# The last 64 tokens of layer 1's attention: from a padded tile of their own rows and columns to units of two halves

## The chip, the core and the metric

The kernel runs on one core of a Trainium2 chip. The metric is the device time of one execution in microseconds (us). The engines that matter are TensorE (PE in the profile, with its weight loads as PEld), VectorE (DVE), ScalarE (ACT), GpSimd (POOL), and SyncE (SP), on whose queue the large transfers are issued. [...]

## The reference

Four layers work on an image batch of 4 x 56 x 56 tokens with 256 channels. Each adds to x what a group-normalised x yields. The change concerns layer 1, whose attention is over all T = 3136 tokens of an image:

```python
xn = x / jnp.maximum(jnp.linalg.norm(x, axis=-1, keepdims=True), EPS)
A = jnp.einsum('bnc,cc,bmc->bnm', xn, W_adj, xn)
A = jnp.exp(5.0 * (A - jnp.max(A, axis=-1, keepdims=True)))
A = A * (1.0 - jnp.eye(n, dtype=A.dtype))
A = A / jnp.maximum(jnp.sum(jnp.abs(A), axis=-1, keepdims=True), EPS)
rowsum = jnp.sum(A, axis=-1, keepdims=True)
xW = jnp.einsum('bnc,dc->bnd', x, W_aff)
Ax = jnp.einsum('bnm,bmc->bnc', A, x)
AxW = jnp.einsum('bnc,dc->bnd', Ax, W_aff)
diff = rowsum * (xW + b_aff) - AxW
...
y = (diff - mu) * jax.lax.rsqrt(var + LN_EPS) * ln_gamma + ln_beta
y = jnp.where(y > 0, y, LEAK * y)
```

W_adj enters by its diagonal alone, so A before its division is symmetric.

## The kernel before

**Tiles.** Tokens are cut into tiles of P = 128. T is 24 whole tiles and 64 tokens more, so NB is 25, and tile 24 is filled up with zeros. Per image the kernel holds `xnT`, the tokens of unit length with channels on partitions (two halves of 128 channels), and `xw`, x times W_aff with tokens on partitions and a 257th column of -1, which yields the row sums.

**Units.** As A is symmetric, only its upper triangle is computed. Row j of tiles runs from tile j to tile 24 in units of up to four tiles (`units`): 25 rows, 91 units and 325 pairs of tiles per image, 300 of them of different tiles. A unit has these steps:

- `logits`: two matmuls (one per channel half, L1377) of up to 512 columns into the PSUM buffer `s`, the exponential on ACT (L1380) into `e`; in a diagonal tile the own token is taken out on POOL (L1382). The stationary side, `xd`, is xnT times the diagonal of W_adj, made on POOL (`scaled`, L1370).
- `transposed`: PE transposes the tiles that are not on the diagonal into `ps_t` (L1391), ACT copies them to `at` (L1394).
- `products`: for each tile two matmuls of 257 columns. `by_row` (L1405) adds to row j's sum in the PSUM buffer `o`. `by_column` (L1410) makes row i's share in the PSUM buffer `v`, which DVE adds to `acc` in SBUF (L1414; in row 0 a copy, L1412). `o`, `s` and `v` have two buffers each.

After a row's last unit `finish` closes the row: DVE adds `o` and `acc` (L1441), divides (L1444, L1446), makes statistics (L1449 to L1451), waits for POOL's power (L1453), scales (L1454), waits for POOL's gamma and beta (L1455, L1456) and applies the leak (L1457). Its second half, `add`, transposes y on PE (L1462) and adds it to the residual (L1470), which is stored when a seventh of the image is complete (L1473).

**Tokens.** `tokens(b, c)` brings in a chunk c of four tiles of image b: load (L1323), normalise (L940), square, `lengths` (L1336, with POOL's power L1339 and the diagonal matrix `dg` L1340), `values` (L1349, evacuated by L953 and L955) and `unit_length` (L1357, then DVE's write of xnT, L1359). Chunk 6 is the 64 tokens alone. Image 0's chunks come first. A later image's chunks are written over those that the rows before have used up: `replace` loads chunk c and puts its steps into the list `small`, from which `small_step` takes one step twice in each unit when it is due; `there` forces the steps of a chunk that the next unit needs. Chunk 6 of an image is replaced in row 0 of that image itself.

**Order.** In layer 1 PE's order is the order of the source. The other engines' orders come from a planner. The main loop works one unit ahead: transposes of unit k, logits of unit k + 1, products of unit k.

```python
            small_step()
            at = transposed(*w, e)
            ...
            if k + 1 < len(units):
                there(units[k + 1][0], units[k + 1][3] - 1)
                ahead = logits(*units[k + 1])
            small_step()
            products(*w, e, at)
            done += last - first
            if last == NB:
                small.append((done + 6, finish(b, j), None))
```

Of the kernel before, what the change touches and what calls it, by code (L numbers as in the profile page):

```python
# [24 lines left out]
FP = mybir.dt.float32  # L25
# [806 lines left out]
def direct_blocks(ctx: ExitStack, tc: tile.TileContext, d: dict, watch):  # L832
# [463 lines left out]

    def layer1(early, big, pool, brief):
        NB = -(-T // P)  # L1300
        real = lambda i: min(P, T - i * P)
        nonlocal m_bufs
        m_bufs, ps_a = 1, ps_m
        w_aff = weight(early, "waff", C)
        acc = big.tile([P, NB, C + 1], FP, name="acc")
        xnT = big.tile([P, CC, NB * P], FP, name="xnT")
        xw = big.tile([P, NB, C + 1], FP, name="xw")
        offd = big.tile([P, P], FP, name="offd")
        nc.vector.tensor_scalar(offd, ident, -1.0, 1.0, ALU.mult, ALU.add)
        nc.vector.memset(xw[:, :, C:], -1.0)  # L1310
        nc.vector.memset(xw[T % P:, NB - 1, :], 0.0)
        nc.vector.memset(xnT[:, :, T:], 0.0)

        def tokens(b, c, ps_a=ps_m):

            tiles = range(4 * c, min(4 * c + 4, NB))
            n = sum(real(t) for t in tiles)
            k, m = real(tiles[0]), len(tiles)
            box = {}

            def load():
                x = early.tile([P, CC, 512], FP, tag="x", name="x1")
                nc.sync.dma_start(out=x[:, :, :n], in_=tokens_of(1, b, 4 * c * P, n))  # L1323
                x1 = box["x"] = early.tile([P, CC, 512], FP, tag="xn", name="xn1")
                sq = box["sq"] = early.tile([P, CC, 512], FP, tag="sq", name="sq", bufs=1)
                for h in range(CC):
                    normalise(x1[:, h, :n], x[:, h, :n], known(1, b), h)
                nc.scalar.activation(sq[:, :, :n], x1[:, :, :n], AF.Square)

            def lengths():  # L1330
                pm, sq = ps_a(), box["sq"]
                rn = early.tile([P, 4, 1], FP, tag="rn", name="rn")
                dg = box["dg"] = early.tile([P, 4, P], FP, tag="dg", name="dg", bufs=1)
                for i, t in enumerate(tiles):
                    for h in range(CC):
                        nc.tensor.matmul(pm[:k, i:i + 1], lhsT=sq[:, h, i * P:i * P + k], rhs=ones[:, 0:1],  # L1336
                                         start=(h == 0), stop=(h == CC - 1))
                nc.vector.tensor_scalar_max(rn[:k, :m, 0], pm[:k, :m], TINY * TINY)
                nc.gpsimd.tensor_tensor(rn[:k, :m, 0], rn[:k, :m, 0], mhalf[:k, 0:1].to_broadcast([k, m]), ALU.pow)  # L1339
                nc.gpsimd.tensor_tensor(  # L1340
                    dg[:k, :m, :k], ident[:k, :k].rearrange("p (o q) -> p o q", o=1).to_broadcast([k, m, k]),
                    rn[:k, :m, :].to_broadcast([k, m, k]), ALU.mult)

            def values(i0):
                pm = ps_a()
                mm = min(2, m - i0)
                for i in range(i0, i0 + mm):
                    for h in range(CC):
                        nc.tensor.matmul(pm[:k, (i - i0) * C:(i - i0 + 1) * C], lhsT=box["x"][:, h, i * P:i * P + k],  # L1349
                                         rhs=w_aff[:, h, :], start=(h == 0), stop=(h == CC - 1))  # L1350
                evac(i0 // 2, xw[:k, 4 * c + i0:4 * c + i0 + mm, :C],
                     pm[:k, :mm * C].rearrange("p (a b) -> p a b", b=C))

            def unit_length():

                pm = ps_a()
                nc.tensor.matmul(pm[:, :n].rearrange("p (m k) -> p m k", k=k), lhsT=ones[:k, :], rhs=box["dg"][:k, :m, :k],  # L1357
                                 start=True, stop=True)
                nc.vector.tensor_tensor(xnT[:, :, 4 * c * P:4 * c * P + n], box["x"][:, :, :n],  # L1359
                                        pm[:, :n].rearrange("p (o k) -> p o k", o=1).to_broadcast([P, CC, n]), ALU.mult)  # L1360

            return [load, lengths] + [lambda i=i: values(i) for i in range(0, m, 2)] + [unit_length]

        xd, out, xr = {}, {}, {}

        def scaled(j):

# [4 lines left out]
        def logits(b, j, first, last):  # L1372

            n = (last - first) * P
            s = psum_tile("s", 2)
            for h in range(CC):
                nc.tensor.matmul(s[:, :n], lhsT=xd[j][:, h, :], rhs=xnT[:, h, first * P:last * P],  # L1377
                                 start=(h == 0), stop=(h == CC - 1))
            e = pool.tile([P, 512], FP, tag="e", name="e1", bufs=3)
            nc.scalar.activation(e[:, :n], s[:, :n], AF.Exp, scale=5.0)  # L1380
            if first == j:
                nc.gpsimd.tensor_tensor(e[:, :P], e[:, :P], offd, ALU.mult)  # L1382
            return e

        def transposed(b, j, first, last, e):
            at = pool.tile([P, 512], FP, tag="at", name="at1")
# [10 lines left out]
        def products(b, j, first, last, e, at):  # L1397
# [10 lines left out]
            def by_column(i):  # L1408
                pv = psum_tile("v", 2)
                nc.tensor.matmul(pv[:, :C + 1], lhsT=e[:, col(i)], rhs=xw[:, j, :], start=True, stop=True)  # L1410
                if j == 0:
                    nc.vector.tensor_copy(acc[:, i, :], pv[:, :C + 1])  # L1412
                else:
                    nc.vector.tensor_tensor(acc[:, i, :], acc[:, i, :], pv[:, :C + 1], ALU.add)  # L1414

            rows = list(range(first, last))
            if first == j:
# [5 lines left out]
            for i in rows:  # L1423
                by_row(i)

        def residual(b, c):

            if (b, c) not in xr and c < NCH:
# [3 lines left out]

        def finish(b, j):

            n = real(j)
            y = pool.tile([P, C + 1], FP, tag="y", name="y", bufs=5)
            u = pool.tile([P, C], FP, tag="u", name="u")
            rd = pool.tile([P, 1], FP, tag="rd", name="rd")
            nc.gpsimd.tensor_tensor(u[:n], xw[:n, j, :C], baff[:n], ALU.add)
            if j:  # L1440
                nc.vector.tensor_tensor(y[:n], out[j][:n, :C + 1], acc[:n, j, :], ALU.add)  # L1441
            else:
                nc.vector.tensor_copy(y[:n], out[j][:n, :C + 1])
            nc.vector.reciprocal(rd[:n], y[:n, C:])  # L1444
            y = y[:n, :C]
            nc.vector.scalar_tensor_tensor(y, y, rd[:n], u[:n], ALU.mult, ALU.add)  # L1446
# [12 lines left out]
            def add():  # L1459
# [5 lines left out]
                while t0 < j * P + n:  # L1465
# [2 lines left out]
                    x = residual(b, c)  # L1468
                    xv = x[:, :, t0 - c * CH:t1 - c * CH]
                    nc.vector.tensor_tensor(xv, xv, pt[:, :, t0 - j * P:t1 - j * P], ALU.add)  # L1470
                    if t1 == (c + 1) * CH:
                        add_stats(2, b, c, x)
                        nc.sync.dma_start(out=tokens_of(2, b, c * CH, CH), in_=x)  # L1473
                    t0 = t1
# [1 line left out]

        NC4 = -(-NB // 4)
        units = [(b, j, i, min(i + 4, NB)) for b in range(NIMG) for j in range(NB) for i in range(j, NB, 4)]  # L1480
        turn = iter(range(4 * NC4))
        fresh = [tokens(0, c, lambda: psum_tile(*(("v", 2), ("o", 2), ("t", 1), ("s", 2))[next(turn) % 4])) for c in range(NC4)]
        for c in range(2):
            fresh[c].pop(0)()
        for c in range(NC4):
            for step in fresh[c]:
                step()
            if c + 2 < NC4:
                fresh[c + 2].pop(0)()
        scaled(0)  # L1490
        e = logits(*units[0])
        small, done = [], 0

        def small_step():
# [3 lines left out]
                    return step()  # L1498
            step_stats()

        def there(b, tile):

            for item in [a for a in small if a[2] == (b, tile // 4)]:
                small.remove(item)
                item[1]()

        def replace(b, c):
            load, *steps = tokens(b, c)
            load()
            at = sum(a[2] is not None for a in small)  # L1510
            small[at:at] = [(done + 8, step, (b, c)) for step in steps]

        for k, w in enumerate(units):
            b, j, first, last = w
            if first == j:
                residual(b, j * P // CH)
                residual(b, j * P // CH + 1)
                if b + 1 < NIMG and j % 4 == 2 and j >= 6:
                    replace(b + 1, j // 4 - 1)
                if b + 1 < NIMG and j == NB - 1:  # L1520
                    replace(b + 1, NC4 - 2)
                if b and j == 0:
                    replace(b, NC4 - 1)
            small_step()
            at = transposed(*w, e)
            if k + 2 < len(units) and units[k + 2][1] == units[k + 2][2]:
                scaled(units[k + 2][1])
            if k + 1 < len(units):
                there(units[k + 1][0], units[k + 1][3] - 1)
                ahead = logits(*units[k + 1])  # L1530
            small_step()
            products(*w, e, at)
            done += last - first
            if last == NB:
                small.append((done + 6, finish(b, j), None))
            e = ahead
        for _, step, _ in small:
            step()
# [491 lines left out]
```

## Time and profile before

| | |
|---|---|
| median of 3 runs | 4114.57 us (4113.07 to 4121.27) |
| profiled execution | 4111.69 us, its span 4109.9 us |
| busy share of the span | PE 95%, PEld 68%, DVE 58%, ACT 33%, POOL 42% |
| mean granted TensorE clock | 0.981 |
| DVE additions to acc (L1414) | 1104, 457.2 us |
| ACT copies of transposes (L1394) | 360, 184.8 us |
| ACT exponentials (L1380) | 364, 200.8 us |

A busy time of PE is the union of its matmuls, whose ends are modelled and overlap. In a group the columns are: line, engine, operation, output and inputs, shape, count, busy time, mean time of one in ns, and the idle time of the engine before them with what ended most of it. In PE's shapes 128*128 stands for rows and columns of the array that an instruction uses. Layer 1 lies between about 825 and 2850 us from the start of the span.

### The profile page before, as it was taken

How to read it: one execution, taken by the hardware profiler on the slowest of the kernel's cores; microseconds unless marked ns; L12 is line 12 of the kernel's file. 1: busy time of each engine (PE TensorE's matmuls, PEld its weight loads, DVE VectorE, ACT ScalarE, POOL GpSimd, SP SyncE). 2: the span in 40 equal slices, each digit the busy share in tenths (PEclk: the TensorE clock that was granted, in tenths of full speed). 3: DMA queues.
4: the chain of work that ended last, by engine and by line, in shares of the span. 5: the costliest groups of instructions: out<-in, count | busy, mean ns of one | idle time of the engine just before them, and what ended most of it. 6: DMA issues, size and time to landing. Idle time of an engine off the chain costs nothing. (4 is left out here: it accounts for less than half of the span.)

```text
span 4109.9 us, 92570 instructions
## 1 busy us (share of the span) xinstructions
PE 3910.4 (95%) x39191; PEld 2788.9 (68%) x39191; DVE 2381.8 (58%) x4437; ACT 1373.1 (33%) x2850; POOL 1741.2 (42%) x1883
## 2 busy tenths in 40 slices
PE   6899999899999999999999999997999999899998
PEld 4566666577777677776777677775666666666665
DVE  6777777734345434454344533444688887666665
ACT  2444545422222122221222212222554555444443
POOL 2566667621123211242112411123676777554544
PEclk9999999999999999999999999998999999999999
DMA  7344333210000100000000000003344443322221
GB/s 261 101 133 122 113 112 101 89 41 10 15 15 24 34 9 15 15 29 29 10 15 15 28 17 10 10 19 117 109 127 121 123 122 112 104 76 73 72 76 61
DMA packets 239794, 275.89 MB, mean 67 GB/s; under 512 B 22150, under 2 KB 231720, under 8 KB 238888
## 3 DMA queue, kind: packets, MB, share of 16 engines
q1 hardware_dynamic: 239082, 269.80, 21.1%
q8 instruction: 310, 5.08, 0.5%
q14 instruction: 114, 0.93, 0.1%
q10 hardware_dynamic: 288, 0.08, 0.0%
HBM read 190.29 MB, written 79.53 MB: 66 GB/s over the span
## 5 line engine op out<-in xcount | busy, mean ns | idle before, releaser
L1414 DVE TENSOR_TENSOR acc<-acc,ps_v 128x257 f32<-128x257 f32 x1104 | 457.2, 421 | 679.5 <-PE ps_v L1410 676.6
L1410 PE MATMUL ps_v<-xw,e 128*128 128x257 f32 x2400 | 666.4, 382 | 27.4 <-DVE acc L1414 17.2
L1405 PE MATMUL ps_o<-xw,at 128*128 128x257 f32 x2400 | 662.5, 380 | 0.0
L1377 PE MATMUL ps_s<-xnT,xd 128*128 128x512 f32 (+3 forms) x1456 | 622.0, 550 | 5.1 <-DVE xnT L1359 5.1
L1410 PEld LDWEIGHTS ps_v<-xw,e 128*128 128x128 f32 x2400 | 445.1, 189 | 193.2 <-issue 91.8
L1394 ACT COPY at<-ps_t 128x512 f32<-128x512 f32 (+3 forms) x360 | 184.8, 513 | 1054.4 <-PE ps_t L1391 1054.4
L1064 POOL TENSOR_TENSOR b<-e 126x336 f32<-126x336 f32 (+5 forms) x512 | 499.7, 997 | 12.1 <-ACT e L1052 4.1
L1405 PEld LDWEIGHTS ps_o<-xw,at 128*128 128x128 f32 x2400 | 455.5, 190 | 65.3
L1370 POOL TENSOR_SCALAR xd<-xnT,vec 128x128 f32<-128x128 f32 x200 | 122.2, 622 | 707.4 <-PE ps_s L1377 705.6
L946 PE MATMUL ps_m<-xn,w_wqkv 128*128 128x392 f32 x1024 | 375.5, 500 | 3.3 <-DVE xr L1693 2.5
L1055 POOL TENSOR_TENSOR e<-e,m0t 126x672 f32<-126x672 f32 (+3 forms) x128 | 238.7, 1865 | 280.7 <-ACT e L1054 267.9
L1377 PEld LDWEIGHTS ps_s<-xnT,xd 128*128 128x128 f32 x1456 | 245.1, 191 | 155.6 <-issue 138.8
L1055 POOL TENSOR_TENSOR e<-e,bias 119x784 f32<-119x784 f32 (+5 forms) x128 | 244.5, 1911 | 215.7 <-ACT e L1054 214.8
L1380 ACT ACTIVATE e<-ps_s 128x512 f32<-128x512 f32 (+3 forms) x364 | 200.8, 552 | 375.2 <-PE ps_s L1377 373.3
L976 ACT ACTIVATE no<-rs 128x168 f32<-128x168 f32 (+2 forms) x256 | 93.8, 367 | 624.7 <-DVE rs L1658 283.1
L1073 PEld LDWEIGHTS ps_o<-e,vp 124*32 124x32 f32 (+3 forms) x8192 | 177.1, 111 | 142.9 <-issue 93.5
L946 PEld LDWEIGHTS ps_m<-xn,w_wqkv 128*128 128x128 f32 x1024 | 188.2, 190 | 124.8 <-ACT pr L1886 17.3
L963 PE MATMUL ps_m<-w_wqkv,xn 128*98 128x256 f32 x1024 | 250.0, 388 | 8.2 <-DMA w_wqkv<-in_wqkv 7.0
L1073 PE MATMUL ps_o<-e,vp 124*32 124x112 f32 (+3 forms) x8192 | 240.2, 254 | 6.2 <-POOL e L1055 4.7
L940 DVE TENSOR_SCALAR xn<-x,gst 128x28 f32<-128x28 f32 (+5 forms) x368 | 204.8, 611 | 50.7 <-PE ps_m L946 26.9
L1052 ACT ACTIVATE e<-e 126x672 f32<-126x672 f32 (+5 forms) x256 | 219.4, 857 | 24.0 <-DVE e L1051 10.7
L965 DVE TENSOR_TENSOR v<-ps_m,bc 98x512 f32<-98x512 f32 (+1 forms) x184 | 126.2, 686 | 174.3 <-PE ps_m L963 98.3
(164 smaller groups left out, 6136.4 us busy)
## 6 DMA issues: line engine op xcount, KB each, us to landing
x<-xr SPq DMA_DIRECT2D x64, 392.0 KB
x<-in_x SPq DMA_DIRECT2D x53, 448.0 KB
xr<-x SPq DMA_DIRECT2D x60, 392.0 KB
x<-x SPq DMA_DIRECT2D x60, 392.0 KB
vd<-v SPq DMA_DIRECT2D x28, 448.0 KB
xr<-in_x SPq DMA_DIRECT2D x32, 392.0 KB
xr<-x SPq DMA_DIRECT2D x28, 448.0 KB
x<-xr SPq DMA_DIRECT2D x28, 448.0 KB
```

What stands on the lines that cost most here:

```text
L940: nc.vector.tensor_scalar(dst, src, gst[:, h, 0:1], gst[:, h, 1:2], ALU.subtract, ALU.mult)
L946: nc.tensor.matmul(pm[:, :n], lhsT=w[:, h, col:col + P], rhs=rhs(h), start=(h == 0), stop=(h == CC - 1))
L963: nc.tensor.matmul(pm[:n, j * C:(j + 1) * C], lhsT=xn[:, h, k * n:(k + 1) * n], rhs=w[:, h, :], start=(h == 0), stop=(h == CC - 1))
L1052: nc.scalar.activation(ev, ev, AF.Exp)
L1055: nc.gpsimd.tensor_tensor(parts(ev), parts(ev), w["emask"], ALU.mult)
L1064: nc.gpsimd.tensor_tensor(w["b"][a][:nk, :, :2 * nq].rearrange("p h (i c) -> p h i c", i=2), ev[:, :, :, 0, :], ev[:, :, :, 1, :], ALU.add)
L1073: nc.tensor.matmul(w["o"](k, i)[j * HD:(j + 1) * HD], lhsT=ones[:nk, :HD] if k else v(j, u), rhs=w["b"][j // 2][:nk, j % 2, i * nq:(i + 1) ...
L1377: nc.tensor.matmul(s[:, :n], lhsT=xd[j][:, h, :], rhs=xnT[:, h, first * P:last * P], start=(h == 0), stop=(h == CC - 1))
L1380: nc.scalar.activation(e[:, :n], s[:, :n], AF.Exp, scale=5.0)
L1405: nc.tensor.matmul(out[j][:, :C + 1], lhsT=e[:, col(i)] if i == j else at[:, col(i)], rhs=xw[:, i, :], start=(i == j), stop=(i == NB - 1))
L1410: nc.tensor.matmul(pv[:, :C + 1], lhsT=e[:, col(i)], rhs=xw[:, j, :], start=True, stop=True)
L1414: nc.vector.tensor_tensor(acc[:, i, :], acc[:, i, :], pv[:, :C + 1], ALU.add)
```

## The change

Rows and units now cover the 24 whole tiles alone (84 units, 276 pairs of different tiles and 24 diagonal ones per image). The 64 tokens are handled *by row* in three units of their own per image, each of which takes eight whole tiles: two halves of four tiles side by side.

- The 64 tokens are loaded twice, so that chunk 6 is a whole tile with two equal halves; `xdr` is its scaled copy. Both halves of `xw` and `xnT` of tile 24 are real data.
- `rest_logits`: half a of the array's columns takes the 64 tokens against tiles 8q + 4a to 8q + 4a + 3. One PSUM buffer holds both, one exponential serves both.
- `rest_transposed`: four transposes, each of which turns two tiles.
- `rest_products`: in four steps, the shares of two tiles (`by_column`'s work, on the two row halves of the array) into both `v` buffers, and the rest's own sums (`by_row`'s work, on the two column halves) into one `o` buffer, whose halves are added later through `racc`.
- `add_up` copies to `acc` at an image's first touch of a tile and adds after that; of the copies of a rest unit the second goes to ACT.
- The last unit also has the 64 tokens among themselves (`own`), and after it `finish(b, NB)` closes their row. Its `add` comes with that of row 23.
- Order: image 0 starts with units 0 and 1 of the rest; those of a later image stand behind rows 20 and 21 of the image before; unit 2 stands behind row 0. `replace` takes chunk 6 at row 3, 0 to 3 at rows 6, 10, 14, 18, 4 at row 20 and 5 at row 22, puts new steps at the head of `small`, and first does what is left of earlier chunks.

```diff
+            if (b, i) in touched:
+                nc.vector.tensor_tensor(acc[:, i, :], acc[:, i, :], pv[:, :C + 1], ALU.add)
+            else:
+                touched.add((b, i))
+                copy(acc[:, i, :], pv[:, :C + 1])
+        def rest_logits(q):
+            s = psum_tile("s", 2)
+            for a in range(2):
+                for h in range(CC):
+                    nc.tensor.matmul(s[a * REST:(a + 1) * REST, :], lhsT=xdr[:, h, a * REST:(a + 1) * REST],
+                                     rhs=xnT[:, h, (2 * q + a) * 512:(2 * q + a + 1) * 512], start=(h == 0), stop=(h == CC - 1))
+            e = pool.tile([P, 512], FP, tag="e", name="e1", bufs=3)
+            nc.scalar.activation(e, s, AF.Exp, scale=5.0)
...
+        def rest_products(b, q, e, own, at):
+            po = psum_tile("o", 2)
+            for i in range(4):
+                pv = [psum_tile("v", 2) for a in range(2)]
+                for a in range(2):
+                    half = slice(a * REST, (a + 1) * REST)
+                    nc.tensor.matmul(pv[a][:, :C + 1], lhsT=e[half, i * P:(i + 1) * P], rhs=xw[half, NB, :], start=True, stop=True)
+                for a in range(2):
+                    add_up(b, 8 * q + 4 * a + i, pv[a], (nc.vector.tensor_copy, nc.scalar.copy)[a])
+                for a in range(2):
+                    nc.tensor.matmul(po[a * REST:(a + 1) * REST, :C + 1], lhsT=at[:, i * P + a * REST:i * P + (a + 1) * REST],
+                                     rhs=xw[:, 8 * q + 4 * a + i, :], start=(i == 0), stop=(i == 3 and (a == 1 or own is None)))
...
+            if q == 0:
+                nc.vector.tensor_copy(racc, po[:, :C + 1])
+            else:
+                nc.vector.tensor_tensor(racc, racc, po[:, :C + 1], ALU.add)
...
+        units = []
+        for b in range(NIMG):
+            if b == 0:
+                units += [(b, None, q) for q in range(2)]
+            for j in range(NB):
+                units += [(b, j, i, min(i + 4, NB)) for i in range(j, NB, 4)]
+                if j == 0:
+                    units.append((b, None, 2))
+                if b + 1 < NIMG and 0 <= j - 20 < 2:
+                    units.append((b + 1, None, j - 20))
...
-                if b + 1 < NIMG and j % 4 == 2 and j >= 6:
-                    replace(b + 1, j // 4 - 1)
-                if b + 1 < NIMG and j == NB - 1:
-                    replace(b + 1, NC4 - 2)
-                if b and j == 0:
-                    replace(b, NC4 - 1)
+                if j in (3, 6, 10, 14, 18, 20, 22):
+                    replace(b + 1, {3: NC4, 20: 4, 22: 5}.get(j, j // 4 - 1))
```

## The prediction

> **What bounds the kernel now.** I read three views first: the busy shares with the 40 slices, then TensorE's share by stretches of layer 1, then the costliest groups. Layer 1 runs from about 825 to 2850 us.
>
> ```profile
> PE   6899999899999999999999999997999999899998
> PEclk9999999999999999999999999998999999999999
> ...
> 850.00:1295.00 445.00, 441.96 (x1941) 329.61 (x1941) 186.24 (x478) 95.57 (x174) 86.47 (x136) 1.00 0.05 15
> 1295.00:1350.00 55.00, 46.82 (x212) 34.43 (x210) 31.07 (x92) 10.46 (x22) 31.63 (x50) 1.00 0.14 43
> 1350.00:1385.00 35.00, 32.10 (x152) 24.72 (x153) 12.35 (x30) 6.56 (x11) 7.51 (x9) 1.00 0.05 16
> 1856.00:1893.00 37.00, 34.80 (x150) 26.82 (x150) 11.58 (x27) 6.63 (x11) 7.42 (x9) 0.91 0.05 15
> ```
>
> The columns of a stretch are its length, the busy time of PE, its weight loads, DVE, ACT and POOL, then the granted clock. In the long rows of an image PE is busy 442 of 445 us: TensorE's own work is the bound. At the passage from image 0 to image 1 (the last short rows and the first row of the next) it idles 8.2 + 2.9 = 11.1 us; the other two passages have the same pattern. At the second and third the clock also falls to 0.91 for 37 us, some 3.3 us each.
>
> ```profile
> L1414 DVE TENSOR_TENSOR acc<-acc,ps_v 128x257 f32<-128x257 f32 x1104 | 457.2, 421 | 679.5 <-PE ps_v L1410 676.6
> L1410 PE MATMUL ps_v<-xw,e 128*128 128x257 f32 x2400 | 666.4, 382 | 27.4 <-DVE acc L1414 17.2
> L1405 PE MATMUL ps_o<-xw,at 128*128 128x257 f32 x2400 | 662.5, 380 | 0.0
> ...
> 1291.27 0.60 PE L1405 MATMUL ps_o<-xw,at 128*128 128x257 f32 x2
> 1291.70 0.59 PE L1410 MATMUL ps_v<-xw,e 128*128 128x257 f32 x2
> ...
> 1299.53 1.88 PE L1377 MATMUL ps_s<-xnT,xd 128*128 128x512 f32 x4
> 1301.25 1.03 PE L1410 MATMUL ps_v<-xw,e 128*128 128x257 f32 x4
> ```
>
> A matmul of the source is two instructions here (x2400 for 4 x 300 pairs of tiles). Durations overlap, so I price by start to start, from the timeline (start, length, engine): 1291.27 to 1291.70 is 0.43 us for one matmul of 257 columns, 1299.53 to 1301.25 is 1.72 for two of 512, that is 0.86 each. DVE waits for PE (677 us), PE for DVE 17.
>
> [...]
>
> ```profile
> 3599.78 1.03 PE L963 MATMUL ps_m<-w_wqkv,xn 128*98 128x256 f32 x4
> 3600.74 0.89 PE L1013 MATMUL ps_o<-e,v 98*32 98x98 f32 x32
> 3601.45 0.86 PE L1013 MATMUL ps_o<-e,ones 98*32 98x98 f32 x32
> 3602.24 0.95 PE L998 MATMUL ps_s<-q,k 32*98 32x98 f32 x32
> 3603.11 1.58 PE L946 MATMUL ps_m<-attn,w_wp 128*128 128x392 f32 x4
> ```
>
> 32 instructions of 98 columns pass in 0.71 us, where the rate above (0.84 ns a column) gives 2.63 one after another: nearly four at once. L963's four of 256 columns should be through 0.85 us after 3599.78, and L1013 starts at 0.96: a change of mode costs 0.11. L998's 32 take 0.87, 0.16 over L1013's 0.71, with the change in and out. I take 0.15 a change, bounds 0.08 and 0.20. [...] Yet the two instructions of one matmul stand on the same quarter, and four quarters still run at once here, so these two at least don't hold the next quarter back. Nothing in this trace has two whole matmuls on one part followed by two on another: whether that holds the logits of the new units back is open. [...]
>
> **The change, part by part.**
>
> *Removed.* Tile 24 as a padded whole tile. A pair of different tiles costs PE: logits 128 columns x 2 channel halves, 4 x 128 x 0.84 ns = 0.43; one transpose 0.11 (three start over 0.33 us, 1293.22 to 1293.55); by_column 0.43; by_row 0.43: 1.40 us. The diagonal one costs 0.43 + 0.43 = 0.86. Per image 24 x 1.40 + 0.86 = 34.5 us go.
>
> *Added.* Three units of eight tiles per image. Logits: four matmuls of 512 columns on 64-column halves. One at a time they cost 4 x 0.86 = 3.44, all two at once 1.72; they are issued half 0, half 0, half 1, half 1[...]. I take 2.15, and 0.15 for the change. Four transposes 0.44 and a change 0.15. Then, four times: two by_column matmuls on row halves at once 0.43, change 0.15, two by_row on column halves at once 0.43, change 0.15: 1.16, in all 4.64. A unit is 2.30 + 0.59 + 4.64 = 7.5 us, three 22.6; the own block adds 4 x 64 x 0.84 ns = 0.22 and 0.58 for its product. So 23.4 instead of 34.5: 11.1 less per image, **44 less in all**. Bounds: changes at 0.08 and logits at 1.72 give a unit of 6.4 and 58 less; no overlap at all gives 3.44 + 0.15 + 0.59 + 4 x 2.02 = 12.3 a unit and 12 *more*.
>
> *Evacuation.* DVE's count hardly moves (276 + 16 + 3 operations for 300, with 8 further copies per image on ACT). But a step now needs both v buffers at once. First pair ends about 0.6 us after its start (the 0.59 of a matmul alone), then one evacuation of 0.42 on DVE, in the first two units beside one on ACT of 0.37 (L1394's 256 columns took that): free at 1.1, in time for the next pair at 1.16. In the third unit both are additions on DVE: 0.6 + 0.84 + 0.05 = 1.5 for the second buffer, so some 0.3 of wait in a step.
>
> *DVE's queue.* It is in order, and a row's finish holds it twice for POOL:
>
> ```profile
> 1296.40 0.57 POOL L1453 TENSOR_TENSOR rstd<-mv,mhalf 128x1 f32<-128x1 f32 x1
> 1297.00 0.41 DVE L1454 TENSOR_SCALAR y<-y,mv,rstd 128x256 f32<-128x256 f32 x1 [1.58 <-POOL rstd L1453]
> 1297.33 0.75 DVE L1414 TENSOR_TENSOR acc<-acc,ps_v 128x257 f32<-128x257 f32 x2
> 1297.79 0.30 PEld L1410 LDWEIGHTS ps_v<-xw,e 128*128 128x128 f32 x2 [1.46 <-DVE acc L1414]
> ```
>
> DVE stands 1.58 us at L1454, the acc additions behind it come late, and PE waits 1.46 for a v buffer. The new program puts each rest unit right behind such a row. For the unit after row 20: the row's chain on DVE is about 2.4 us of operations, POOL's rstd, L1454, to about 3.6 after the row's last product; the first copy follows to 4.0; then L1457, which waits for gamma and beta on POOL (0.73 each), to 5.7, and the second copy. PE arrives for its second pair at 3.1 and its third at 5.1: about 0.9 + 1.0 lost. After row 21 the chain is followed by xnT (L1359, 1.22), and the second pair waits from 4.9 to 7.0: 2.1. Rows 22 and 23 have finishes back to back, and the next image's first unit waits about 0.7 for its exponential and 1.5 for v buffers. Sum 6 in place of 11: the forced token steps of chunk 6, which cost 2.9 in the second stretch above, move to where they have cover (chunk 5 is loaded at row 22 and written two units before it is read). **15 less over three passages**; bounds 5 and 20. The third unit comes behind row 0's finish and wants additions: first step 0.5, second 1.5, then 0.3 each: 2.5 more, **10 in all**, bounds 4 and 16.
>
> *Start.* Image 0 now begins with rest units, which need xdr: xnT of the last chunk (0.29) and two POOL products (0.62 each by L1370) stand between L1357 and the first logits, where row 0's logits now start at once: **1.8 more**, once. What follows is order without cost: SP issues two loads of 64 tokens per image where it issued one, all of them rows ahead (x's buffers are free early; DVE sat in the short rows for PE and POOL, not for DMA). The end of layer 1 keeps its form: last finish, additions, store, layer 2's load behind it on SP.
>
> *Clock.* The two falls to 0.91 follow a PE wait of some 3 us. With the longest near 2 they may go: between 0 and 6.6, I take **3.3 less**.
>
> Sum: -44 - 15 + 10 + 1.8 - 3.3 = -51. The profiled execution took 4111.69 us (span 4109.9 and 1.8 around it): 4061. The median of three, 4114.57, stands 2.9 above it, so I say **4064**, and give the rivals on the median too.
>
> **Rivals.**
> 1. *The halves don't overlap* (the change doesn't do what it says). +12, passages -15, third unit +5 as longer units hide more, start +2: +4, 4119. For: quarters are all that the trace shows overlapping. Against: with quarters it works in rows and columns alike.
> 2. *Evacuation sets the pace.* Steps of 1.7 instead of 1.16 as two buffers and one round trip close a loop, logits at 3.0: unit 10.5, 2.1 less per image, -8 - 15 + 10 + 2 = -11: 4104. For: the third unit's arithmetic. Against: the ACT share.
> 3. *Slower: the finish chain holds every rest unit.* Place: DVE's in-order queue at L1454 and L1457, waiting for POOL. In the trace one chain ran 6.3 us (L1441 at 1293.20 to L1457's end at 1299.48). If POOL, which also has tokens' pow (1.02), dg (1.04) and xd there, is late by 3 more, DVE frees the second pair at 9.3 where PE wants it at 3.1: 6.2 a unit, 12 units = 74, against 44 of gain; nothing gained at the passages or by the clock: +30, start +2, 4147. It decides from 3.7 us of wait a unit on average (11.1 / 3). Against: POOL is 57% busy even in the short rows, and image 0's first two units have no finish before them.
> 4. *Better*: logits fully two at once, changes at 0.08, passages -20, third unit +4, clock -6.6, start +2: -79, 4036.
>
> **How the numbers follow.** Mine 0.62, spread 4042 to 4092; rival 1 0.10, rival 2 0.12, rival 3 0.09, rival 4 0.07. The range 4034 to 4112 leaves out rival 3, most of rival 1 and a part of rival 4, 0.19. Within 0.2% (8 us) counts as same, about what a measurement of this kernel can tell. Faster: 0.62 + 0.07 + three quarters of rival 2 and a little of rival 1 = 0.79. Slower: rival 3 and a third of rival 1 = 0.12. Same: 0.09.
>
> **What would show it.** In the new timeline, by_column of a rest unit (form 64*128) should start in pairs within some 20 ns, by_row (128*64) too, with 0.1 to 0.2 between the two forms. A unit from its transposes to its last product should span 6 to 10 us, with PE waits for DVE acc or for ACT of 2 us once a unit, none above 3. PE's idle time at a passage should be near 6 us, the clock 1.00. The groups of whole tiles of L1410 and L1405 fall from 2400 to 2208 instructions. If pairs start 0.43 apart, rival 1 holds; if PE idles 4 us or more in every rest unit, rival 3.

## The result and the profile after

| | before | after |
|---|---|---|
| median of 13 runs | 4113.82 us | 4097.55 us |
| lowest to highest | 4104.31 to 4121.96 | 4085.04 to 4102.80 |
| profiled execution, its span | 4111.69, 4109.9 us | 4100.35, 4098.3 us |
| of the span: layer 1, from its first matmul to the end of its last | 2029.8 us | 2009.6 us |
| mean granted TensorE clock | 0.981 | 0.973 |

The ratio is 0.9955, with a 95% interval of 0.9943 to 0.9966: 16 us less, where 50 were forecast. The other layers, whose code the change leaves alone, took 2080.1 and 2088.8 us of the two profiled executions (2076 to 2089 over all eight traces of this study), so I read layer 1 for itself: 20.2 us less.

The slices of the page after:

```profile
PE   6899999899999999999999999997999999899998
PEclk9899999999999999999999999998999999999999
```

In layer 1 (slices 9 to 28) they look as they did before: differences of a few us don't show there. The stretches of the kernel after, one for each image (the last ends at 2780) and one for the first passage, have the columns of those before: length, busy time of PE, PEld, DVE, ACT and POOL, the granted clock, then the DMA share and GB/s.

```profile
825.00:1325.00 500.00, 489.79 (x2207) 359.13 (x2206) 211.70 (x537) 106.63 (x196) 117.64 (x177) 0.99 0.07 22
1325.00:1825.00 500.00, 487.85 (x2163) 353.06 (x2163) 221.06 (x579) 105.00 (x196) 122.36 (x191) 0.98 0.06 19
1825.00:2325.00 500.00, 487.21 (x2161) 353.89 (x2161) 220.58 (x577) 104.93 (x196) 122.02 (x190) 0.98 0.06 20
2325.00:2780.00 455.00, 445.69 (x1970) 321.46 (x1970) 198.36 (x520) 94.65 (x178) 103.44 (x165) 0.99 0.05 16
1290.00:1400.00 110.00, 101.44 (x469) 68.89 (x468) 50.63 (x139) 22.43 (x46) 42.09 (x64) 0.95 0.09 27
```

The same stretches of the kernel before:

```profile
825.00:1325.00 500.00, 493.46 (x2204) 371.21 (x2205) 213.87 (x541) 107.39 (x193) 113.65 (x171) 1.00 0.06 19
1325.00:1825.00 500.00, 488.96 (x2167) 364.91 (x2166) 218.52 (x576) 105.88 (x195) 121.26 (x189) 1.00 0.06 20
1825.00:2325.00 500.00, 487.50 (x2147) 363.90 (x2146) 218.46 (x573) 102.94 (x190) 118.19 (x185) 0.99 0.06 20
2325.00:2780.00 455.00, 444.30 (x1931) 330.10 (x1930) 194.38 (x513) 94.16 (x176) 103.32 (x164) 0.99 0.04 14
1290.00:1400.00 110.00, 98.54 (x453) 73.38 (x452) 53.77 (x146) 21.46 (x42) 42.22 (x65) 1.00 0.12 36
```

PE's busy time hardly differs. That tells little, for a matmul is busy longer at half clock (four instructions of `by_row` in a rest unit are 0.66 us at a clock of 1.00 and 1.12 at 0.50, in the timelines below): the column to read is the clock, which is lower by 0.01 to 0.02 in the first three images, with 0.95 in the passage. Added up over the trace's clock records, layer 1 before spends 13.6 us at half clock (the two falls that the prediction speaks of, 6.8 us each), layer 1 after 57.9 us, in ten places of 3.4, 6.8 or 13.7 us. Some 10 us at the end of layer 1, which every trace of this study has, are left out of all these sums.

The costliest groups of the page after that answer to those of before, and the groups of the rest units (shapes kept apart):

```profile
L1399 DVE TENSOR_TENSOR acc<-acc,ps_v 128x257 f32<-128x257 f32 x1104 | 455.9, 421 | 687.1 <-PE ps_v L1476 671.0 <-PE ps_v L1438 13.6
L1476 PE MATMUL ps_v<-xw,e 128*128 128x257 f32 x2208 | 613.0, 382 | 19.4 <-DVE acc L1399 17.7 <-DVE mv L1517 1.7
L1471 PE MATMUL ps_o<-xw,at 128*128 128x257 f32 x2208 | 608.9, 379 | 0.0
L1438 PE MATMUL ps_v<-xw,e 64*128 64x257 f32 x192 | 46.1, 506 | 19.6 <-DVE acc L1402 11.1 <-DVE acc L1399 8.5
L1442 PE MATMUL ps_o<-xw,at 128*64 128x257 f32 x192 | 39.3, 495 | 0.0
```

In the kernel after `by_column` of the whole tiles is L1476, `by_row` L1471; in the rest units they are L1438 and L1442, and DVE adds at L1399 and copies at L1402. As foreseen, 192 of 2400 instructions went from each of the two large groups. Idle time ahead of `by_column` rose from 27.4 us (L1410 of before) to 19.4 + 19.6 = 39.0: the rest units brought waits of their own, 11.1 us for copies and 8.5 us for additions.

PE's timeline of a rest unit with no row's finish ahead of it (start, length; its transposes began at 878.55):

```profile
880.84 0.70 PE L1438 MATMUL ps_v<-xw,e 64*128 64x257 f32 x4
881.47 0.66 PE L1442 MATMUL ps_o<-xw,at 128*64 128x257 f32 x4
882.05 0.70 PE L1438 MATMUL ps_v<-xw,e 64*128 64x257 f32 x4
```

A step is 0.63 + 0.58 = 1.21 us for four matmuls that would take 4 x 0.43 = 1.72 one by one: two at a time, with 0.2 and 0.15 over the 0.43 of one matmul. These I put down to the changes between row and column halves; nothing shows them apart. From its transposes to the next unit's the unit took 7.16 us; the logits in this stretch are those of the next unit, 1.82 us of whole tiles, about as long as a rest unit's own (1.88, from 871.22 to 873.10).

The timeline of unit 2 of image 1, behind the finish of row 0, DVE beside PE:

```profile
1422.61 0.41 DVE L1520 TENSOR_SCALAR y<-y,mv,rstd 128x256 f32<-128x256 f32 x1 [0.68 <-POOL rstd L1519]
1423.01 0.41 DVE L1399 TENSOR_TENSOR acc<-acc,ps_v 128x257 f32<-128x257 f32 x1
1425.21 0.66 DVE L1523 SCALAR_TENSOR_TENSOR y<-y 128x256 f32<-128x256 f32 x1 [1.79 <-POOL y L1522]
...
1426.26 1.22 PE L1438 MATMUL ps_v<-xw,e 64*128 64x257 f32 x2 [2.08 <-DVE acc L1399]
1427.41 1.12 PE L1442 MATMUL ps_o<-xw,at 128*64 128x257 f32 x4
1428.46 1.23 PE L1438 MATMUL ps_v<-xw,e 64*128 64x257 f32 x4
1429.62 1.13 PE L1442 MATMUL ps_o<-xw,at 128*64 128x257 f32 x4
```

And the stretches around that wait:

```profile
1424.00:1426.00 2.00, 0.17 (x1) 0.00 (x0) 0.79 (x2) 0.00 (x0) 1.93 (x4) 1.00 0.00 0
1426.00:1432.70 6.70, 6.44 (x22) 2.39 (x22) 2.47 (x7) 0.00 (x0) 0.00 (x0) 0.50 0.01 2
```

DVE stands at the finish's last operation, L1523 (L1457 of before), for gamma and beta on POOL; PE stands 2.08 us for the addition behind it; and then the clock is 0.50 for 6.7 us, and each part of a step takes 1.05 to 1.16 us where it took 0.63 or 0.58. Of the ten units that follow a finish, each with a wait of 1.6 to 2.3 us, eight have such a fall in them or right behind. Of the two other places one is the start, in a wait of 2.3 us. The other, at 1350.9, has no wait in the 3.4 us ahead of it: PE worked a rest unit's last products and then `lengths`, 16 matmuls of one column each in 1.95 us (L1342).

### The profile page after: what moved, and what is told of

Its sections match the earlier page's. It is cut to its first block, busy times and chain, and to the rows that moved or that the text cites. A ratio compares the mean times of both kernels' runs of the same rounds, so it can differ in the third digit from the quotient of the medians.

```text
span 4098.3 us, 92479 instructions
## 1 busy us (share of the span) xinstructions
PE 3893.5 (95%) x39143; PEld 2735.2 (67%) x39143; DVE 2379.5 (58%) x4419; ACT 1369.6 (33%) x2854; POOL 1741.0 (42%) x1883
## 4 chain that ended last, share of the span: by engine, by line
PE 47%; DVE 4%; POOL 2%; issue 1%; DMA 1%; ACT 0%; SPq 0%; POOLq 0%; DVEq 0%; ACTq 0%
PE ps_m L946 12%; PE ps_o L1471 6%; PE ps_s L1387 6%; PE ps_v L1476 6%; PE ps_m L963 5%; PE ps_o L1073 3%; PE ps_s L1044 2%; PE ps_o L1013 2%; PE ps_t L1457 1%; PE ps_s L998 1%; DVE rs L1744 1%; DMA x<-x 1%; PE ps_m L1355 0%; DVE e L1051 0%; DVE xn L940 0%
## 5 line engine op out<-in xcount | busy, mean ns | idle before, releaser
L1399 DVE TENSOR_TENSOR acc<-acc,ps_v 128x257 f32<-128x257 f32 x1104 | 455.9, 421 | 687.1 <-PE ps_v L1476 671.0
L1476 PE MATMUL ps_v<-xw,e 128*128 128x257 f32 x2208 | 613.0, 382 | 19.4 <-DVE acc L1399 17.7
L1471 PE MATMUL ps_o<-xw,at 128*128 128x257 f32 x2208 | 608.9, 379 | 0.0
L1387 PE MATMUL ps_s<-xnT,xd 128*128 128x512 f32 (+3 forms) x1344 | 572.3, 548 | 0.0
L1476 PEld LDWEIGHTS ps_v<-xw,e 128*128 128x128 f32 x2208 | 408.7, 189 | 170.4 <-issue 80.4
L1460 ACT COPY at<-ps_t 128x512 f32<-128x512 f32 (+3 forms) x332 | 170.0, 512 | 998.8 <-PE ps_t L1457 998.5
L1471 PEld LDWEIGHTS ps_o<-xw,at 128*128 128x128 f32 x2208 | 419.2, 190 | 60.0
L1387 PEld LDWEIGHTS ps_s<-xnT,xd 128*128 128x128 f32 x1344 | 226.0, 191 | 135.3 <-issue 126.7
L1390 ACT ACTIVATE e<-ps_s 128x512 f32<-128x512 f32 x336 | 185.4, 552 | 334.2 <-PE ps_s L1387 333.1
L946 PEld LDWEIGHTS ps_m<-xn,w_wqkv 128*128 128x128 f32 x1024 | 189.0, 191 | 125.3 <-ACT pr L1972 17.1
```

The costliest lines, as they stand in the source:

```text
L946: nc.tensor.matmul(pm[:, :n], lhsT=w[:, h, col:col + P], rhs=rhs(h), start=(h == 0), stop=(h == CC - 1))
L1471: nc.tensor.matmul(out[j][:, :C + 1], lhsT=e[:, col(i)] if i == j else at[:, col(i)], rhs=xw[:, i, :], start=(i == j), stop=(i == NB - 1))
```

## The experiments

The theory: the matmul work shrank as predicted, and about 40 us of it were given back through the waits of the rest units for their evacuation, half as idle time and half as the half clock that follows. Rivals: evacuation in general sets the pace of the units; the start costs the difference; PE's work is simply larger than I worked out. The number of the kernel before was 4112.74 us beside the first four runs and 4113.27 beside the last two.

### Unit 2 away from the finish

```diff
-                units += [(b, j, i, min(i + 4, NB)) for i in range(j, NB, 4)]
-                if j == 0:
-                    units.append((b, None, 2))
+                row = [(b, j, i, min(i + 4, NB)) for i in range(j, NB, 4)]
+                if j == 1:
+                    row.insert(3, (b, None, 2))
+                units += row
```

> Unit 2 of the rest stands inside row 1, after its third unit, so no row's finish is on DVE ahead of it. Theory (a finish chain on DVE holds the evacuation, and the wait makes the clock fall): the wait of 2.3 to 2.8 us in the second pair of these four units goes, and the half-clock stretches of 3.4 to 6.8 us that follow them (at about 928, 1426, 1931 and 2426 us) go with it; 11 us of waits and some 8 of clock, so about 4079 us. Rival (using half of the array lowers the clock, waits or not): the waits go, the half-clock stretches stay: about 4087. Rival (the chain only moves to the next place that wants DVE): no change from 4097.

Measured: 4074.83 us, ratio 0.9905 (0.9893 to 0.9918); layer 1 took 1990.2 us, 19.3 less than after the change. The rest units' `by_column` in its trace:

```profile
L1438 PE MATMUL ps_v<-xw,e 64*128 64x257 f32 x192 | 41.8, 466 | 12.0 <-DVE acc L1402 12.0
```

The waits for additions, 8.5 us, are gone, and the units' products at half clock with them (46.1 to 41.8 here, 39.3 to 34.7 us in L1442): some 17 of the 19 us. Layer 1's time at half clock fell to 34.1 us, and none of it stands behind unit 2. Both of unit 2's evacuations are still additions on DVE, and steps take 1.21 and 1.54 us in turn. So evacuation in general costs 0.3 us in every second step; it is the finish ahead that costs 2 us and the clock.

### Both copies of a rest unit on ACT

```diff
-                    add_up(b, 8 * q + 4 * a + i, pv[a], (nc.vector.tensor_copy, nc.scalar.copy)[a])
+                    add_up(b, 8 * q + 4 * a + i, pv[a], nc.scalar.copy)
```

> In the first-touch copies of units 0 and 1 ACT makes both copies, DVE none; nothing else differs. Theory: these copies no longer queue behind L1520 and L1523 on DVE, so the 2.2 us wait in the units behind rows 20 and 21 (six units) goes, for about 0.3 us a step as ACT copies two in series (0.37 each); the half-clock stretches at 1344, 1351, 1368, 1846 and 2368 us (27 us in sum) shrink: 13 - 7 + 10 = 16 less, about 4081. Rival (it is the mode, not the wait): the falls stay, 4091. Rival (the waits are not DVE's): 4097.

Measured: 4071.01 us, ratio 0.9904 (0.9891 to 0.9917); layer 1 1983.1 us, 26.5 less than after. The unit behind row 20 in its timeline, where DVE stands for the same finish as before:

```profile
1337.33 0.65 PE L1442 MATMUL ps_o<-xw,at 128*64 128x257 f32 x4
1337.43 0.65 ACT L1402 COPY acc<-ps_v 128x257 f32<-128x257 f32 x2
1337.92 0.92 PE L1438 MATMUL ps_v<-xw,e 64*128 64x257 f32 x4
1338.65 0.65 ACT L1402 COPY acc<-ps_v 128x257 f32<-128x257 f32 x2 [0.57 <-PE ps_v L1438]
1338.67 0.54 DVE L1520 TENSOR_SCALAR y<-y,mv,rstd 128x256 f32<-128x256 f32 x1 [1.59 <-POOL rstd L1519]
1338.77 0.65 PE L1442 MATMUL ps_o<-xw,at 128*64 128x257 f32 x4
```

DVE's 1.59 us at L1520 no longer reaches PE, as ACT frees both buffers (two copies in 0.65 us). Half clock in layer 1 fell to 17.1 us: what is left stands at the start and behind the four units 2, which still wait. The kernel after had split the evacuation between ACT and DVE, with 11.1 us of waits for copies: a step needs both buffers, so the half that stays in DVE's queue holds both. With both copies on ACT none of these is left (8.5 us remain, for unit 2's additions). The place in the queue decided, not the capacity.

### The start inside row 0

Image 0's units 0 and 1 stand behind row 0's second and fourth unit.

```diff
-            if b == 0:
-                units += [(b, None, q) for q in range(2)]
...
+                if b == 0 and j == 0:
+                    row[4:4], row[2:2] = [(b, None, 1)], [(b, None, 0)]
...
+        scaled(0)
```

> Image 0 starts with row 0 and has units 0 and 1 of the rest inside it, so that the first logits no longer wait for xnT and xdr of the last chunk. Theory: the waits before the first logits fall from 2.4 + 1.7 to some 2 us and the 6.8 us at half clock from 863 on, which cover those logits, go: 2 + 3 = 5 less, 4092. Rival (the start is hidden by work that is due anyway, or DVE's additions in row 0 now hold PE): 4097 or more.

Measured: 4092.77 us, ratio 0.9956 (0.9943 to 0.9968), which by these intervals can't be told from the kernel after (0.9955); layer 1 2006.4 us, 3.2 less. The number of the forecast was met, its way only in part: the wait for `xdr` (1.4 us) went, but the wait of 2.3 us before it and the clock's fall there stayed (10.2 us at half clock from 857.7, where it was 6.8). The start is not where the prediction was missed.

### All three

> The three edits together. If they act on separate waits the gains add up: 18 + 16 + 5, about 4058 us, and layer 1's time at half clock falls from 58 us (44 more than before the change) to 15 or less. If the clock falls anyway: about 4075, with the half-clock time still above 40 us.

Measured: 4055.36 us, ratio 0.9865 (0.9849 to 0.9881), the shortest time of all: 57 us below the kernel before, where the change as it stands is 16 below. Layer 1 took 1968.9 us, 40.7 less than after; one by one the three brought 19.3 + 26.5 + 3.2 = 49, so they share a part. The rest units' groups in its trace:

```profile
L1438 PE MATMUL ps_v<-xw,e 64*128 64x257 f32 x192 | 39.9, 429 | 0.0
L1442 PE MATMUL ps_o<-xw,at 128*64 128x257 f32 x192 | 31.4, 406 | 0.0
```

PE's waits at the first passage (in total, times, the longest), here and then in the kernel after:

```profile
PE ps_v L1476 <- DVE acc L1399: 4.0, 4, 1.5
PE ps_m L1363 <- POOL rstd L1519: 1.0, 1, 1.0
```

```profile
PE ps_v L1476 <- DVE acc L1399: 3.6, 3, 1.5
PE ps_v L1438 <- DVE acc L1402: 3.2, 2, 1.6
PE ps_m L1363 <- POOL rstd L1519: 1.0, 1, 1.0
```

The rest units' 19.6 us of waits are 0.0, their products' busy time is 71.3 instead of 85.4 us: 33.7 of the 40.7. Layer 1 is 60.9 us shorter than before the change. Half clock in layer 1 is down to 13.6 us, as long as before the change: 10.2 at the start and 3.4 at 1826.1. The predicted gain was there, and the waits of the rest units, with the clock, had taken most of what was missing. PE's work is therefore not larger than I worked out. What stays at the passage are the waits of the short rows themselves.

### Filling the wait with useless work

To part the clock from the idle time, two matmuls of 512 columns stand ahead of the second step of the ten units that follow a finish. Nobody reads what they write; nothing else changes.

```diff
+                if i == 1 and (b or q == 2):
+                    fill = psum_tile("t", 1)
+                    for h in range(CC):
+                        nc.tensor.matmul(fill, lhsT=ident, rhs=xnT[:, h, :512], start=(h == 0), stop=(h == CC - 1))
```

> The changed kernel with two matmuls of 512 columns more (1.72 us) ahead of the second pair of by_column in each of the ten rest units that have a finish chain ahead; their output is read by nobody. Theory (the wait lowers the clock, and this costs as much as the wait): TensorE works where it waited, so the second pair starts no later; the half-clock stretches behind these units (51 us) go for the most part: 15 to 22 us less, about 4078, though 17 us of work are added. Rival (only the waits count, the clock costs nothing as it falls in idle time): 4097 to 4105. Rival (using half of the array lowers the clock): half-clock time stays at some 58 us, about 4100.

Measured: 4075.12 us, ratio 0.9908 (0.9895 to 0.9922); layer 1 1991.3 us. Ten times two matmuls of 0.86 are 17 us more for PE, and the kernel is 22 us faster (layer 1 18). Two images and the first passage in the stretches of its trace, then its group of rest `by_column` (L1442 here), and unit 2 of image 1 in its timeline, where L1438 is the fill:

```profile
1325.00:1825.00 500.00, 492.34 (x2207) 357.59 (x2206) 224.93 (x586) 106.21 (x198) 124.46 (x193) 1.00 0.07 20
1825.00:2325.00 500.00, 492.34 (x2203) 356.89 (x2203) 223.32 (x587) 106.51 (x199) 125.29 (x195) 1.00 0.06 20
1290.00:1400.00 110.00, 103.75 (x488) 70.83 (x487) 53.29 (x142) 23.58 (x47) 40.34 (x61) 1.00 0.11 32
```

```profile
L1442 PE MATMUL ps_v<-xw,e 64*128 64x257 f32 x192 | 39.0, 429 | 2.9 <-DVE acc L1402 1.6 <-DVE acc L1399 1.2
```

```profile
1411.20 1.98 PE L1438 MATMUL ps_t<-xnT,ident 128*128 128x512 f32 x4
1413.11 0.70 PE L1442 MATMUL ps_v<-xw,e 64*128 64x257 f32 x2
1414.22 0.70 PE L1442 MATMUL ps_v<-xw,e 64*128 64x257 f32 x2 [0.41 <-DVE acc L1399]
```

The second half of the pair still comes late, as DVE's queue is what it was (it starts 1.11 us behind the first); but the long wait is full of work, the clock of these stretches is 1.00, and half clock in layer 1 goes from 57.9 to 10.2 us. The waits went from 19.6 to 2.9 us, which is the 17 that the fill takes: that is even, and the 18 to 22 us gained are the clock's, more than the 16 us that the change brought. The work on array halves is the same here and in the kernel with all three edits, and nearly all the falls are gone (10.2 and 13.6 us at half clock, from 57.9): halves alone don't lower the clock, the waits had a part in it. Idleness is not all of it either. Besides the start's, one fall is left here, at 1836.5 us, and PE was busy in the 3.4 us ahead of it (`lengths` is L1342; then the stretches before and behind the fall):

```profile
1834.69 1.95 PE L1342 MATMUL ps_m<-ones,sq 128*128 128x1 f32 x16
```

```profile
1833.10:1836.50 3.40, 3.40 (x29) 2.31 (x25) 1.16 (x3) 0.67 (x2) 0.00 (x0) 1.00 0.00 0
1836.50:1839.90 3.40, 3.40 (x12) 1.01 (x11) 0.16 (x1) 1.32 (x2) 2.06 (x2) 0.51 0.00 0
```

The fall at 1826.1 in the kernel with all three edits has the same place, between `lengths` and the logits of the next rest unit, and no wait. So a stretch in which PE is busy with very small matmuls was followed by a fall as a wait was. The fill is work on the whole array; how much it owes to that was not tried.

### Units inside long rows

Like the kernel with all three edits, but units 0 and 1 of the next image stand inside rows 13 and 19, with more work around them.

```diff
-                if b + 1 < NIMG and 0 <= j - 20 < 2:
-                    units.append((b + 1, None, j - 20))
...
+                if b + 1 < NIMG and j == 13:
+                    row.insert(2, (b + 1, None, 0))
+                if b + 1 < NIMG and j == 19:
+                    row.insert(1, (b + 1, None, 1))
```

> As the kernel with all three edits, but units 0 and 1 of the images 1 to 3 stand inside the longer rows 13 and 19 of the image before instead of behind rows 20 and 21. Theory: with no finish chain in their way the place of the units is worth little; the short rows lose their cover, which was worth about 1 to 3 us a passage: 4058 to 4065 against 4055. Rival (the place among the short rows is what gains): a passage goes back to 11 us of waits with a fall of the clock: 4075 or more.

Measured: 4091.68 us, ratio 0.9951 (0.9935 to 0.9967), 36 us slower than the kernel with all three edits; my theory fell here. Its first passage in stretches, and three of PE's waits from 1300 to 1400, none of which the kernel with all three edits has at that passage:

```profile
1290.00:1330.00 40.00, 35.14 (x146) 25.15 (x144) 17.91 (x50) 7.18 (x13) 14.55 (x23) 0.89 0.07 23
1330.00:1380.00 50.00, 42.70 (x187) 28.18 (x187) 24.26 (x66) 10.40 (x24) 22.40 (x36) 0.95 0.12 35
```

```profile
PE ps_m L1355 <- DVE rn L1344: 1.9, 1, 1.9
PE ps_m L1363 <- DVE xw L953: 1.8, 2, 0.9
PE ps_m L1355 <- ACT xw L955: 1.4, 2, 0.7
```

The rest units themselves have no wait here either, but the next image's tokens run back to back, twice. The unit in row 19 needs chunk 3, which is loaded only at row 18, so `begin` forces its steps (lengths, values, unit length, 1318 to 1330 us). And the load of chunk 5 at row 22 forces those of chunk 4 (1355 to 1368), as they are due only eight tiles after their load and rows 20 and 21 have seven (with the two rest units it was fifteen). In the kernel with all three edits such steps stand between other units there, and PE waits 1.0 us for them at that passage. The clock falls here as well: 37.5 us at half clock in layer 1, against 13.6; the first fall, 10.2 us from 1321.5, stands behind `lengths` with 0.8 us of waits around it, the second behind the wait of 1.9 us. So units among the short rows seem to be cover for the tokens there, if they don't wait themselves; but the edit also made chunk 3 due too early, and how much of the 36 us is the one and how much the other was not separated.

## Why the prediction was wrong

The sign and the range (4034 to 4112) held, the size did not. In the prediction's own order, against layer 1's 20.2 us:

- *Matmul work, -44*: right. A unit was forecast at 7.5 us and measured 7.16 undisturbed, twelve of them 4 us better, which makes -48 (worked out, not measured as a whole). A step was forecast at 1.16 (0.43 and 0.15 twice) and measured 1.21. The logits, taken at 2.15 (an estimate: half a matmul of 0.86 over the 1.72 of full overlap, as the issue order half 0, half 0, half 1, half 1 might hold them back), took 1.88 from their start to the next instruction's.
- *Third unit, +10*: right in size, 8.5 us of waits in four units, nearly all in the second step.
- *Start, +1.8*: the waits there rose from 1.3 to 3.7 us, +2.4.
- *Passages, -15*: too much. PE's idle time at the three passages (1290 to 1400, 1790 to 1905 and 2295 to 2410) was 11.5, 11.4 and 11.1 us before and 8.6, 9.2 and 9.7 after, 6.5 less in all. At the first the units' own waits (3.2 us) were near those forecast for rows 20 and 21 (0.9 + 1.0 and 2.1); the v buffers of whole tiles cost 3.6 us where 1.5 was forecast, and the wait of `unit_length` (1.0) was left out. One reading of mine was off there too: the 1.46 us of wait for a v buffer are the weight load's, PE's own wait at that place (1297.79 in the kernel before) is 1.05.
- *Clock, -3.3*: this is the step that failed. "With the longest near 2 they may go": instead the time at half clock went from 13.6 to 57.9 us, up to 22 us lost (an estimate: half of the 44 us more). I had seen two falls behind waits of some 3 us and made a threshold of it between 2 and 3, though the same wait at the first passage (2.97 us, to 1350.80) had none behind it. The waits of 1.6 to 2.3 us in the rest units, which I had forecast near their size and priced as idle time only, had falls behind them in eight units of ten. The bounds, 0 to 6.6 in the good direction, had no room for a loss.

The sum of these terms is -48 + 8.5 + 2.4 - 6.5 + 22 = -21.6, against -20.2; as near as a sum with two estimates in it can be expected to come. Of the 34 us by which the medians' difference missed the forecast (16 less instead of 50), the clock's term is some 25 and the passages' 8.5.

Of the rivals, the first fell (the halves do overlap); the second comes near in time, but the undisturbed units ran at 1.21 a step; the third had the mechanism, the finish chain in DVE's queue holding the rest unit, at some 2 us a unit instead of 6.2. Its point of decision, 3.7 us of wait a unit, counted idle time alone; with the clock the ten units lost 19.6 + 14 us in products, 3.4 each, close to it.

## What to carry to other kernels

A wait of the engine that bounds the kernel may have to be priced twice: its own length, and the slower clock behind it, which here cost about as much again (19.6 us of waits in the rest units; with 17 us of work in their place the kernel was 22 us faster). If work goes into a stage where its evacuation stands in a queue behind a chain that waits itself (an addition behind DVE's wait of 1.79 us for POOL kept PE for 2.08), put its evacuation on an engine that doesn't stand in that chain, for both buffers that a step needs, or put the work where no chain ends. Before moving units out of a stage with many small round trips, ask what they covered, and what their new place makes due earlier.

## What was not expected of the hardware

- Waits of 1.6 to 2.3 us in rest units had a fall of the clock to half behind them in eight cases of ten, for 3.4, 6.8 or 13.7 us. At 1424 a wait of 2.08 us had 6.7 us at a clock of 0.50 behind it, with steps on array halves on both sides of it.
- Between `products` of whole tiles a wait of 1.74 us had no fall behind it: the kernel before has one at each passage (the first is below), and its clock stays 1.00 for 28 us or more after each. That speaks for the lighter steps on halves having a part, as does the fall behind `lengths` without a wait; neither was tried by itself. Rest units without a wait kept full clock (1.00 from 1410 to 1440 with all three edits, where PE is busy throughout), but for some with `lengths` right behind them (3.4 us at half clock at 1826.1 there).

```profile
1323.23 0.70 PE L1410 MATMUL ps_v<-xw,e 128*128 128x257 f32 x2 [1.74 <-DVE acc L1414]
```

- Useless matmuls can pay: 17 us of them made the kernel 22 us faster.
- Matmuls on two column halves, issued two and two, ran at once but for 0.16 us: 1.88 for four, where two of whole tiles take 1.72.
